# Summing the weighted values of a graph convolution on TensorE instead of halving them on VectorE, with a reordered step and more buffers in the expert FFN

## The chip, the cores and the metric

The kernel runs on one core of one Trainium2 chip. The core has the engines that the profile names PE (TensorE, matrix products), DVE (VectorE), ACT (ScalarE), POOL (GpSimd) and SP (SyncE, which here only issues transfers), and sixteen DMA engines. The metric is the device time of one launch in microseconds; the time given is the median of several runs.

## The reference

The program is a two-layer graph network on 3125 nodes of 256 features and 100,000 edges, all in fp32. Each layer adds a graph convolution and a mixer to the nodes and then a feed-forward part. Layer 0, cut to what matters here:

```python
def transformer_conv(x, edge_index, wq, bq, wk, bk, wv, bv, ws, bs, heads, out_ch):
    ...
    qi, kj, vj = (q[dst], k[src], v[src])
    alpha = jnp.sum(qi * kj, axis=-1) / math.sqrt(out_ch)
    amax = jax.lax.stop_gradient(jax.ops.segment_max(alpha, dst, num_segments=n))
    ex = jnp.exp(alpha - amax[dst])
    denom = jax.ops.segment_sum(ex, dst, num_segments=n)
    alpha = ex / denom[dst]
    out = jax.ops.segment_sum(vj * alpha[..., None], dst, num_segments=n)
    out = out.reshape(n, heads * out_ch)
    return out + x @ ws + bs
...
h = transformer_conv(x, edge_index, w1q, ...)
h = leaky_relu(batch_norm(h, g1, be1))
h = transformer_conv(h, edge_index, w2q, ...)
...
topk_vals, topk_idx = jax.lax.top_k(gate_logits, K)      # 16 experts, K = 2
topk_w = jax.nn.softmax(topk_vals, axis=-1)
h = jax.nn.relu(jnp.einsum('bsh,ehf->bsef', x, w1) + b1)
expert_out = jnp.einsum('bsef,efh->bseh', h, w2) + b2
sel = jnp.take_along_axis(expert_out, topk_idx[:, :, :, None], axis=2)
y = x + jnp.sum(topk_w[..., None] * sel, axis=2)
return (y - mu) / jnp.sqrt(var + EPS) * gamma + beta     # mu, var: of y, per row
```

So for every node, each of its incoming edges fetches the key and the value of its source node; a softmax over the node's edges (4 heads of 64) weighs the values, and the weighted values are summed. This is done twice, with a batch norm between. Independently of it a mixer of four layers (linear attention, then an MLP of 256 to 1024 to 256) runs on the same normalized input. The two results are added to x, and each row goes to its two best experts.

## The kernel before, in words

**The convolution.** Nodes are sorted by their number of edges into 25 blocks of 128 (one node per partition). A block has as many slots as its busiest node has edges: `SLOTS` (L627) lists 64, 43, 41 down to 22, 833 in all. `steps` (L912) cuts a block into sub-blocks of at most `SUB` = 8 slots (L630) and pairs them into steps; over both convolutions there are 126 steps and 230 sub-blocks, 80 of 8 slots, 126 of 7 and 24 of 6. `SlotOrder` (L1063) does the work of a step:

- `gathers` (L1076): one indirect DMA by POOL per slot (issued in `gather`, L635) brings 128 rows of key and value from `kvtab` into `kv`; the pool of `kv` has four buffers, two steps' worth, and gathers run one step ahead.
- `keys`: DVE multiplies keys by the query (L1114) and reduces (L1117); `softmax` and `exp` (L1141, ACT) make the weights.
- `values` (L1147 to L1158): DVE multiplies the values by the weights (L1153) and then adds the second half of the sub-block's slots onto the first (L1158).
- `sums` (L1160): PE adds what is left by matmuls with the identity, which accumulate in the PSUM tile `cps` (L1168) over all sub-blocks of a step:

```python
left = [*range(m // 2), *range(m // 2 * 2, m)]
for j in left:
    self.k.nc.tensor.matmul(
        t["acc"][:, :D], self.k.ident, kv[:, j, D:], start=(b0 + j == 0),
        stop=(b == len(t["subs"]) - 1 and j == left[-1]),
    )
```

  So 8 slots take 4 matmuls, 7 take 4 and 6 take 3.
- `result` copies the sum out (L1175, ACT); `join` and its parts put a block's steps together.

**The order.** PE, DVE and ACT run this stage in an order written out by hand (`PATTERN`, L1060, under `manual_schedule`, L1364): the letters are the parts above, and at each of three `m` per step a `Filling` (L838) puts in pieces of the mixer's work, measured out by their PE time. `l0_gnn_slots` (L1318) runs the two convolutions and tells the filling how many such points there are. While the mixer is in an attention part, few matmuls and much DVE work lie beside the convolution; in an MLP part (L1855, L1873), many matmuls. The same sum in layer 1 (`by_slots`, L942, halves at L1020 and matmuls at L1023) is a function of its own.

**The expert FFN** (`l0_ffn_routed`, L2034). For seven groups of up to four tiles of 125 tokens, the gate's logits, the two best experts and the place of each token in its expert's list are worked out (slot numbers `sloti`, L2132). Then 50 indirect DMAs by POOL scatter the tokens' rows to the experts' lists `xs` in DRAM (L2135); a zero fill of `xs` comes before them. The normed rows `acc` are made with gamma, and beta is added to `xcur` by seven POOL instructions (L2148), which the scheduler put ahead of the scatters. The loop over 16 experts (L2152 on) waits for all scatters (`after`, L291, adds a wait by hand), loads `xe`, transposes it, multiplies by the two weights and writes the rows `ys`. In the combine each token tile gathers its two result rows (`g`, L635, from a pool `f_back` of 8 buffers), DVE adds them with their weights (L2196) and normalizes, and the group is stored (`x`, rows, columns) with the layer-1 keys and values (`st`, L2220, stored to `kvtab` by SP).

Of the kernel before, what the change touches and what calls it, by code (L numbers as in the profile page):

```python
# [14 lines left out]
ALU = mybir.AluOpType  # L15
# [4 lines left out]
P = 125  # L20
D = 256
# [269 lines left out]
def after(k, ins, others):  # L291

    for other in others:
        k.tc.add_manual_dep(
            ins.ins, other.ins.name,
            mybir.DependencyInfo(mybir.DependencyClass.Sync, mybir.DependencyReason.DATA),
            reason="rows of the table",
        )
# [295 lines left out]
def l0_gnn(k, x, conv, y_mix, xcur):  # L594
# [32 lines left out]
SLOTS = [  # L627
    64, 43, 41, 39, 38, 37, 36, 35, 35, 34, 33, 33, 32, 32, 31, 30, 30, 29, 29, 28, 27, 26, 25, 24, 22
]
# [282 lines left out]
def steps(ns):  # L912

    n = -(-ns // SUB)
    subs = [ns // n + (i < ns % n) for i in range(n)]
    return [subs[i : i + 2] for i in range(0, n, 2)]
# [146 lines left out]
class SlotOrder:  # L1063
# [79 lines left out]
    def values(self, n, b):  # L1143

        nc, t, H = self.k.nc, self.steps[n], self.HEADS
        if b == 0:
            nc.vector.tensor_reduce(  # L1147
                self.tile(t["i"])["den"][:, t["c"]], t["w"].rearrange("p s h -> p h s"), axis=AX.X,
                op=ALU.add,
            )  # L1150
        m, kv, b0 = t["subs"][b], t["kv"][b], sum(t["subs"][:b])
        v = self.heads(kv[:, :m, D:])
        nc.vector.tensor_tensor(  # L1153
            v, v, t["w"][:, b0 : b0 + m].unsqueeze(3).to_broadcast([128, m, H, D // H]), op=ALU.mult
        )
        half = m // 2
        v = kv[:, :half, D:]
        nc.vector.tensor_tensor(v, v, kv[:, half : 2 * half, D:], op=ALU.add)  # L1158

    def sums(self, n, b):  # L1160

        t = self.steps[n]
        m, kv, b0 = t["subs"][b], t["kv"][b], sum(t["subs"][:b])
        if b == 0:
            t["acc"] = self.pp.tile([128, 512], F32, name="cps", tag="cps")
        left = [*range(m // 2), *range(m // 2 * 2, m)]
        for j in left:
            self.k.nc.tensor.matmul(  # L1168
                t["acc"][:, :D], self.k.ident, kv[:, j, D:], start=(b0 + j == 0),
                stop=(b == len(t["subs"]) - 1 and j == left[-1]),  # L1170
            )

    def result(self, n):
# [144 lines left out]
def l0_gnn_slots(k, dram, order, a, y, pp, pq, cw, filling, tmp):  # L1318
# [4 lines left out]
    nc, N = k.nc, k.N  # L1323
    NQ = len(SLOTS)
# [7 lines left out]
    with ExitStack() as st:  # L1332
# [11 lines left out]
        for g0, ng in k.groups:  # L1344
            t = wp.tile([P, 4, 2 * D], F32, name="st", tag="st")
# [14 lines left out]
    bmv = cw.tile([128, 2, 2], F32, name="bmv")  # L1360
    sc = cw.tile([128, 2], F32, name="sc")
    sh = cw.tile([128, 2], F32, name="sh")
    mix = filling(2 * 3 * sum(len(steps(n)) for n in SLOTS) + NQ)
    with k.tc.manual_schedule(engines=ORDERED):  # L1364
        mix.ahead(30.0)
        prev = None
        for n in (1, 2):
            if n == 2:
                weights = l0_qs_weights(k, cw, a, 2)
            wq, bq, wsk, bs, gam, bet = weights  # L1370
# [85 lines left out]
            with ExitStack() as st:  # L1456
# [4 lines left out]
                sent, ps = [], None  # L1461
                norm_cols(k, h[:, 0], h[:, 0], sc, sh)
                for i in range(NQ):
# [8 lines left out]
                    if n == 1:  # L1472
                        mix(0.3)
                        t = wp.tile([128, 2 * D], F32, name="kvrow", tag="kvrow")
                        nc.vector.tensor_tensor(t, ps, bkv, op=ALU.add)
                        put_rows(k, kvtab2, order, i, t, sent)
                    else:
                        t = wp.tile([128, D], F32, name="row", tag="row")
# [434 lines left out]
def layer0(k, dram, x, order_of, a, y):  # L1913
# [3 lines left out]
    with ExitStack() as st:  # L1917
        wts, one, mwp, hp, hp2, cw, pp, cp, pq = pools(
            k, st,
            [("m_w", 1), ("m_one", 1), ("m_work", 1), ("m_hid", 1), ("m_hT", 2), ("c_w", 1)],  # L1920
            [("m_ps", 4), ("c_ps", 2), ("c_qa", 2)],
        )
        for g0, ng in k.groups:
            nc.sync.dma_start(y[:, g0 : g0 + ng], tok(x)[:, g0 : g0 + ng])
        tmp = ExitStack()
        order = order_of(pools(k, tmp, [("n_one", 1), ("n_wk", 4)]), cp)
        with ExitStack() as s2:
            (wp,) = pools(k, s2, [("m_ln", 1)])
            mv, rs = ln_stats(k, wp, y)
            for i in range(NT):  # L1930
                ln_tile(k, y[:, i], y[:, i], mv, rs, i)
        pieces = l0_mix_pieces(k, dram, sub("L0_mix_"), y, wts, one, mwp, hp, hp2, pp)
        gout, sent = l0_gnn_slots(
            k, dram, order, sub("L0_gnn_"), y, cp, pq, cw, lambda n: Filling(pieces, n), tmp
        )
        (wp,) = pools(k, st, [("c_add", 2)])
        for g0, ng in k.groups:
            xt = wp.tile([P, 4, D], F32, name="xt", tag="xt")
            part = wp.tile([P, 4, D], F32, name="part", tag="part")
            nc.sync.dma_start(xt[:, :ng], tok(x)[:, g0 : g0 + ng])  # L1940
            after(k, nc.sync.dma_start(part[:, :ng], tok(gout[0:k.N, :])[:, g0 : g0 + ng]), sent)
            nc.gpsimd.tensor_tensor(xt[:, :ng], xt[:, :ng], part[:, :ng], op=ALU.add)
            nc.vector.tensor_tensor(y[:, g0 : g0 + ng], y[:, g0 : g0 + ng], xt[:, :ng], op=ALU.add)
# [90 lines left out]
def l0_ffn_routed(k, dram, xcur, a, over, a1):  # L2034
# [4 lines left out]
    nc, N, NT = k.nc, k.N, k.NT  # L2039
# [9 lines left out]
    with ExitStack() as st:  # L2049
        big, one, wts, wp, gp, bp, hp, pp = pools(  # L2050
            k, st,
            [("f_big", 1), ("f_one", 1), ("f_w", 3), ("f_wk", 3), ("f_g", 2), ("f_back", 8), ("f_hid", 2)],
            [("f_ps", 2)],
        )
        zero = big.tile([128, 4 * D], F32, name="zero")
# [9 lines left out]
        bet = one.tile([P, D], F32, name="bet")  # L2065
# [23 lines left out]
        sent = []  # L2089
        for g0, ng in k.groups:  # L2090
# [7 lines left out]
            for j in range(ng):  # L2098
                at = ps[:P, j * NE : j * NE + NE]
                for c in range(2):  # L2100
                    m = nc.tensor.matmul(
                        at, xT[:, c, j * P : j * P + P], gw[:, c, :], start=(c == 0), stop=False
                    )
# [29 lines left out]
            for i in range(g0, g0 + ng):  # L2133
                for r in range(2):
                    ins = nc.gpsimd.indirect_dma_start(  # L2135
                        out=xs, in_=acc[:, i], in_offset=None,
                        out_offset=bass.IndirectOffsetOnAxis(ap=sloti[:, r, i : i + 1], axis=0),
                    )
# [6 lines left out]
        nc.vector.tensor_reduce(over[:P, 0:1], full, axis=AX.X, op=ALU.max)  # L2145
        for g0, ng in k.groups:
            x = xcur[:, g0 : g0 + ng]
            nc.gpsimd.tensor_tensor(x, x, bet.unsqueeze(1).to_broadcast([P, ng, D]), op=ALU.add)  # L2148

        b1 = one.tile([128, NE, 4], F32, name="b1")  # L2150
        nc.sync.dma_start(b1, a["b1"].rearrange("e (c p) -> p e c", p=128))
# [38 lines left out]
        for gi, (g0, ng) in enumerate(k.groups):  # L2190
# [25 lines left out]
            t = gp.tile([P, 4, 2 * D], F32, name="st", tag="st")  # L2216
# [1051 lines left out]
def fast(k, dram, a, out, over, dump):  # L3268

    sub = lambda pre: {s[len(pre) :]: v for s, v in a.items() if s.startswith(pre)}  # L3270

    def show(name, xcur):
        if dump is not None and name in dump:
            k.nc.sync.dma_start(tok(dump[name]), xcur)

    with ExitStack() as st:
        (keep,) = pools(k, st, [("order", 1)])
        order_of = lambda tmp, pp: node_order(
            k, dram, a["src"], a["dst"], keep, tmp, pp, over[:, 0:2]
        )  # L3280
        with ExitStack() as s2:
            (xpool,) = pools(k, s2, [("xcur", 1)])
            xcur = xpool.tile([P, k.NT, D], F32, name="xcur")
            order = layer0(k, dram, a["x"], order_of, a, xcur)
            show("x1", xcur)
            tabs = l0_ffn_routed(k, dram, xcur, sub("L0_ffn_"), over[:, 2:3], sub("L1_gnn_"))
            show("x2", xcur)
        layer1(k, dram, a, out, tabs, order, show)
# [56 lines left out]
```

## Time and profile before

| what | value |
|---|---|
| median of 9 runs | 6414.68 us (6391.49 to 6472.89) |
| profiled execution | 6413.31 us, span 6411.5 us |
| busy share of the span | PE 74%, DVE 68%, POOL 46%, ACT 25% |
| granted TensorE clock, mean | 0.821 of full speed |
| layer 0, convolutions and mixer | about 285 to 3145 us |
| layer 0, beta and routing, scatters | about 3240 to 3370 us |
| layer 0, experts | 3375 to 3620 us |
| layer 0, combine | 3620 to 3793 us, layer 1 behind it |

A group's line gives the line of code, engine, operation, tile written and read, shapes and count; then busy time and the mean of one in ns; then the engine's idle time just before these instructions and what ended most of it. A timeline line gives the start, the duration, the instruction, and in brackets the idle time before it and its releaser. A matmul of fp32 leaves two records, so counts of matmuls in the profile are twice those of the code, and a run of equal matmuls is shown as one line.

### The profile page before, as it was taken

The numbers are of one execution on the slowest core, as the hardware profiler recorded it, in microseconds if no ns is written. First come the engines' busy times: TensorE is split into PE (matmuls) and PEld (weight loads), VectorE is DVE, ScalarE is ACT, GpSimd is POOL, SyncE is SP. The second block draws the span as 40 slices with busy tenths as digits, with TensorE's granted clock in tenths as the row PEclk, the third lists the DMA queues.
The fourth block names the chain that finished last, engine by engine and source line by source line (L and its number), as shares of the span: only waits on it lengthen the run. The fifth ranks groups of instructions, "written<-read, shape, count | busy, mean of one in ns | idle before, by whom it ended". The sixth has DMA issues, their size and how long they took to land. (4 is left out here: it accounts for less than half of the span.)

```text
span 6411.5 us, 48523 instructions
## 1 busy us (share of the span) xinstructions
PE 4740.5 (74%) x15769; PEld 2716.3 (42%) x15769; DVE 4364.0 (68%) x6216; ACT 1584.7 (25%) x3284; POOL 2936.0 (46%) x2945
## 2 busy tenths in 40 slices
PE   3367887688856787678749747787887877787768
PEld 2144554455434555456436423333333333333335
DVE  5287878888488777988531346567777666777657
ACT  1032333322323223322311102222221222221222
POOL 2465665666366565666450233334334434334321
PEclk8687988789878888789859867788887888788879
DMA  5366665666366565666444353334444434344320
GB/s 139 92 180 180 185 184 154 182 190 179 127 176 186 169 177 166 177 188 182 130 143 144 121 182 108 106 107 127 121 121 131 119 112 116 109 121 132 115 68 22
DMA packets 374280, 908.49 MB, mean 142 GB/s; under 512 B 94268, under 2 KB 170074, under 8 KB 373892
## 3 DMA queue, kind: packets, MB, share of 16 engines
q0 software_dynamic: 232624, 725.48, 39.4%
q1 hardware_dynamic: 137412, 168.23, 8.1%
q10 hardware_dynamic: 3982, 11.59, 0.5%
q8 instruction: 128, 2.10, 0.1%
q14 instruction: 134, 1.10, 0.1%
HBM read 813.62 MB, written 91.30 MB: 141 GB/s over the span
## 5 line engine op out<-in xcount | busy, mean ns | idle before, releaser
L635 POOL DMA_INDIRECT kv<-kvtab,slots x2499 | 2462.2, 985 | 2148.6 <-PE acc L1023 859.0
L2599 DVE TENSOR_TENSOR kv<-kv,e 128x1024 f32<-128x1024 f32 (+1 forms) x448 | 504.8, 1139 | 428.7 <-PE e L2594 191.7
L2594 PE MATMUL e<-weT,eaT 128*128 128x512 f32 (+1 forms) x896 | 558.9, 722 | 184.5 <-ACT eaT L2593 102.6
L1168 PE MATMUL cps<-kv,ident 128*128 128x256 f32 x1792 | 527.5, 445 | 134.9 <-DVE kv L1158 70.1
L1114 DVE TENSOR_TENSOR kv<-kv,qa 128x1792 f32<-128x1792 f32 (+2 forms) x230 | 478.7, 2081 | 95.6 <-DMA kv<-kvtab,slots 66.2
L1168 PEld LDWEIGHTS cps<-kv,ident 128*128 128x128 f32 x1792 | 393.2, 226 | 282.0 <-issue 121.2
L1117 DVE TENSOR_REDUCE al<-kv 128x28 f32<-128x1792 f32 (+2 forms) x230 | 479.5, 2085 | 7.9
L1153 DVE TENSOR_TENSOR kv<-kv,qa 128x1792 f32<-128x1792 f32 (+2 forms) x230 | 477.3, 2075 | 0.0
L1873 PE MATMUL mm<-w,hid 128*125 128x256 f32 x1600 | 414.4, 406 | 69.8 <-ACT hid L1863 39.4
L1855 PE MATMUL mm<-hTm,w 128*128 128x500 f32 (+1 forms) x896 | 394.2, 583 | 75.3 <-issue 38.7
L1873 PEld LDWEIGHTS mm<-w,hid 128*125 128x125 f32 x1600 | 309.9, 200 | 156.2 <-issue 65.2
L2594 PEld LDWEIGHTS e<-weT,eaT 128*128 128x128 f32 (+1 forms) x896 | 164.7, 222 | 426.6 <-issue 233.1
L1023 PE MATMUL acc<-kv,ident 128*128 128x256 f32 x896 | 262.7, 456 | 60.5 <-DVE kv L1020 55.5
L1855 PEld LDWEIGHTS mm<-hTm,w 128*128 128x128 f32 x896 | 169.7, 205 | 242.8 <-issue 189.8
L1023 PEld LDWEIGHTS acc<-kv,ident 128*128 128x128 f32 x896 | 203.4, 232 | 142.7 <-DVE kv L1020 87.1
L1545 PE MATMUL mm<-ident,xh 125*128 125x125 f32 x400 | 109.6, 370 | 201.5 <-ACT xh L1535 111.3
L2593 ACT COPY eaT<-e 128x128 f32<-128x128 f32 (+1 forms) x448 | 109.8, 267 | 557.6 <-PE e L2591 281.3
L1158 DVE TENSOR_TENSOR kv<-kv 128x768 f32<-128x768 f32 (+1 forms) x230 | 242.0, 1052 | 7.9
L985 DVE TENSOR_TENSOR kv<-kv,qa 128x1792 f32<-128x1792 f32 (+2 forms) x115 | 238.9, 2078 | 5.0 <-issue 3.8
L989 DVE TENSOR_REDUCE al<-kv 128x56 f32<-128x1792 f32 (+2 forms) x115 | 238.8, 2077 | 5.1 <-issue 4.2
L1014 DVE TENSOR_TENSOR kv<-kv,al 128x1792 f32<-128x1792 f32 (+2 forms) x115 | 235.1, 2082 | 0.0
L2591 PE MATMUL e<-ident,ea 128*128 128x128 f32 (+1 forms) x448 | 133.3, 329 | 97.0 <-issue 41.9
(414 smaller groups left out, 7952.8 us busy)
## 6 DMA issues: line engine op xcount, KB each, us to landing
kv<-kvtab,slots POOLq DMA_INDIRECT x2499
w<-in_L_ffn_w_dram SPq DMA_DIRECT2D x32, 512.0 KB
qd<-qT SPq DMA_DIRECT2D x24, 500.0 KB
kvtab<-st SPq DMA_DIRECT2D x12, 1000.0 KB
qT<-qd SPq DMA_DIRECT2D x24, 500.0 KB
xTg<-xcols SPq DMA_DIRECT2D x24, 500.0 KB
w<-in_L_mix_W_dram SPq DMA_DIRECT2D x8, 1024.0 KB
xs<-zero SPq DMA_DIRECT2D x16, 512.0 KB
```

Source lines behind the costliest of these rows:

```text
L635: return k.nc.gpsimd.indirect_dma_start(out=out, out_offset=None, in_=table, in_offset=bass.IndirectOffsetOnAxis(ap=index, axis=0),)
L985: nc.vector.tensor_tensor(kv[:, :m, :D], kv[:, :m, :D], q.unsqueeze(1).to_broadcast([128, m, D]), op=ALU.mult,)
L1023: nc.tensor.matmul(acc[:, :D], k.ident, kv[:, j, D:], start=(b0 + j == 0), stop=(kv is bufs[-1][2] and j == left[-1]),)
L1114: nc.vector.tensor_tensor(kv[:, :m, :D], kv[:, :m, :D], q.unsqueeze(1).to_broadcast([128, m, D]), op=ALU.mult)
L1117: nc.vector.tensor_reduce(t["al"][:, b0 : b0 + m], self.heads(kv[:, :m, :D]), axis=AX.X, op=ALU.add)
L1153: nc.vector.tensor_tensor(v, v, t["w"][:, b0 : b0 + m].unsqueeze(3).to_broadcast([128, m, H, D // H]), op=ALU.mult)
L1158: nc.vector.tensor_tensor(v, v, kv[:, half : 2 * half, D:], op=ALU.add)
L1168: self.k.nc.tensor.matmul(t["acc"][:, :D], self.k.ident, kv[:, j, D:], start=(b0 + j == 0), stop=(b == len(t["subs"]) - 1 and j == left[-1]),)
L1855: nc.tensor.matmul(ps[:, :w_], W["w1"][:, c, j * 128 : j * 128 + 128], o["hT"][:, c, :w_], start=(c == 0), stop=(c == 1),)
L1873: nc.tensor.matmul(ps[:P, :D], s["hid"][:, c, j * P : j * P + P], W["w2"][:, c, :], start=(c == 0), stop=False,)
L2594: nc.tensor.matmul(e[:, :n].rearrange("p b d -> p (b d)"), eaT[r], weT[r, :n].rearrange("p b d -> p (b d)"), start=True, stop=True,)
L2599: nc.vector.tensor_tensor(t, t, e[:, :n].unsqueeze(2).to_broadcast([128, n, 2, D]), op=ALU.add)
```

## The change

```diff
@@ values
-        half = m // 2
-        v = kv[:, :half, D:]
-        nc.vector.tensor_tensor(v, v, kv[:, half : 2 * half, D:], op=ALU.add)
@@ sums
-        left = [*range(m // 2), *range(m // 2 * 2, m)]
-        for j in left:
+        for j in range(m):
             self.k.nc.tensor.matmul(
                 t["acc"][:, :D], self.k.ident, kv[:, j, D:], start=(b0 + j == 0),
-                stop=(b == len(t["subs"]) - 1 and j == left[-1]),
+                stop=(b == len(t["subs"]) - 1 and j == m - 1),
             )
@@ l0_gnn_slots
-    mix = filling(2 * 3 * sum(len(steps(n)) for n in SLOTS) + NQ)
+    mix = filling(2 * 3 * sum(len(steps(n)) for n in SLOTS) + 1 * NQ)
@@ l0_ffn_routed
-            [("f_big", 1), ("f_one", 1), ("f_w", 3), ("f_wk", 3), ("f_g", 2), ("f_back", 8), ("f_hid", 2)],
+            [("f_big", 1), ("f_one", 1), ("f_w", 3), ("f_wk", 3), ("f_g", 2), ("f_back", 14), ("f_hid", 2)],
@@ l0_ffn_routed
-            nc.gpsimd.tensor_tensor(x, x, bet.unsqueeze(1).to_broadcast([P, ng, D]), op=ALU.add)
+            ins = nc.gpsimd.tensor_tensor(
+                x, x, bet.unsqueeze(1).to_broadcast([P, ng, D]), op=ALU.add
+            )
+            after(k, ins, sent[-1:])
```

The weighted values of all of a sub-block's slots go to PE, and no halves are added on DVE. Of the number of filling points only the spelling changes. In the FFN the pool of gathered result rows has fourteen buffers, and each beta add waits for the last scatter.

In the compiled program PE, DVE and ACT keep their order of instructions otherwise; DVE has 230 fewer, PE 770 more matmuls (1666 instead of 896). On POOL the seven beta adds stand behind the fifty scatters and behind a partition all-reduce, with the library switch that used to come before an iota of layer 1 now ahead of them. Two POOL gathers of layer 1's edge features (`ea`), issued among the combine's 50 gathers, stand behind 26 and 30 of them instead of 16 and 20, and the first 14 gathers have no wait for a buffer, where 8 had none.

## Prediction

> **What bounds the kernel now.** I read the share of busy time, then the windows by stage, the waits inside layer 0, and single timeline rows. Most of the change lies in layer 0's two convolutions with the mixer beside them (300 to 3140 us). Its windows (columns: us, busy and count of PE, PEld, DVE, ACT, POOL, then PE clock, DMA share, GB/s):
>
> ```profile
> 300.00:600.00 300.00, 193.97 (x672) 129.47 (x672) 245.53 (x335) 89.12 (x199) 184.13 (x184) 0.76 0.61 178
> 600.00:1000.00 400.00, 341.87 (x1296) 233.31 (x1296) 330.38 (x436) 119.70 (x219) 257.59 (x261) 0.91 0.63 182
> 1000.00:1300.00 300.00, 205.70 (x749) 138.86 (x748) 256.90 (x392) 98.86 (x227) 176.37 (x178) 0.78 0.60 174
> 1300.00:1640.00 340.00, 283.80 (x1011) 187.30 (x1009) 273.80 (x357) 90.23 (x159) 221.28 (x223) 0.89 0.62 180
> 1780.00:2100.00 320.00, 210.05 (x752) 139.71 (x753) 272.94 (x378) 103.69 (x235) 194.33 (x193) 0.79 0.61 179
> 2100.00:2470.00 370.00, 302.24 (x1146) 207.53 (x1145) 282.81 (x362) 107.09 (x187) 217.95 (x222) 0.88 0.60 174
> 2470.00:2820.00 350.00, 253.69 (x915) 170.25 (x914) 306.84 (x448) 118.81 (x273) 210.48 (x210) 0.82 0.60 176
> 2820.00:3140.00 320.00, 265.85 (x967) 179.41 (x966) 252.03 (x331) 90.99 (x161) 187.85 (x188) 0.89 0.59 172
> 800.00:900.00 100.00, 89.12 (x337) 60.16 (x335) 85.92 (x111) 29.19 (x49) 66.43 (x68) 0.95 0.64 181
> ```
>
> Two kinds of stretch alternate with the mixer's layers. **A**, beside attention (300, 1000, 1780, 2470; 1270 us): PE 863 busy (68%), DVE 1082 (85%). **B**, beside the mixer's MLP (the other four; 1430 us): PE 1194 (83%), DVE 1139 (80%). The last line is the stage's densest 100 us: PE 89%, clock 0.95. Neither engine is full; they hand sub-blocks to each other:
>
> ```profile
> POOL kv L635 <- PE cps L1168: 323.7, 69, 17.8
> PEld cps L1168 <- DVE kv L1158: 92.6, 37, 12.9
> DVE kv L1114 <- DMA kv<-kvtab,slots: 66.2, 23, 20.0
> ```
>
> (us, times, longest; window 300 to 3140.) Gathers wait for the sums to free a buffer, DVE only 66 us for gathers. The page's chain of waits ends its walk about 5.12 ms, after this stage, so I followed releasers back by the page's rule from the stage's last work. Of 2840 us: PE 943, DVE 902, issue 404, POOL 186, ACT 151. The sums (L1168) have 71 of their 239.9 busy us on it in A (30%) and 157 of 281.8 in B (56%); the halves (L1158) 42 of 106.9 in A and 35 of 132.4 in B.
>
> **The change, part by part.**
>
> ```profile
> L1168 PE MATMUL cps<-kv,ident 128*128 128x256 f32 x1792 | 527.5, 445 | 134.9 <-DVE kv L1158 70.1
> L1158 DVE TENSOR_TENSOR kv<-kv 128x768 f32<-128x768 f32 (+1 forms) x230 | 242.0, 1052 | 7.9
> 837.58 1.89 PE L1168 MATMUL cps<-kv,ident 128*128 128x256 f32 x8
> 839.31 1.84 PE L1855 MATMUL mm<-hTm,w 128*128 128x500 f32 x4
> 1102.96 3.78 PE L1168 MATMUL cps<-kv,ident 128*128 128x256 f32 x8 [1.78 <-DVE kv L1158]
> 1106.53 1.40 PE L1419 MATMUL cps<-ident,res 128*128 128x128 f32 x6
> ```
>
> (1) *Sums.* A matmul leaves two records, so 1792 records are 896 matmuls. The 230 sub-blocks (80 of 8 slots, 126 of 7, 24 of 6) go from 4, 4, 3 matmuls to 8, 7, 6: 320 + 378 + 72 = 770 more. By 384 recorded matmuls in A and 500 in B these split 330, 430 and 10 elsewhere. Price: start to next start of four is 839.31 - 837.58 = 1.73 us, 0.43 each, at full clock, and 1106.53 - 1102.96 = 3.57, 0.89, at half. Group means: 0.625 in A, 0.563 in B. Added PE: 142 (0.43) to 206 (0.625) in A, 185 to 242 in B.
>
> (2) *Halves.* 230 DVE instructions go: 106.9 us in A, 132.4 in B. The instruction order of PE, DVE and ACT is otherwise unchanged.
>
> (3) *On the path.* B, by shares: 56% of 185 to 242 is 104 to 136, less the halves' 35: +69 to +101. B, by room: if PE reaches the densest window's 89%, (1194 + 185) / 0.89 = 1549, +119; with the old busy also shrinking to that window's clock, (1194 x 0.893 / 0.95 + 185) / 0.89 = 1469, +39 (0.893: B's mean clock). I take **+75**, near the shares' lower end, since added matmuls follow one another without a wait. A: 30% of 142 to 206 is 43 to 62, less 42: +1 to +20; DVE loses its part while PE has 407 idle us there, so I take **0**. Bounds for A: -107 (every half on the path, no sum on it) to +62 (the reverse). For B: -35 to +183, (1194 + 242) / 0.89.
>
> The clock's records here stand at 0.5 or 1.0 only, averaging 0.76 to 0.82 in A and 0.88 to 0.91 in B, 0.99 in the experts' stage (PE 98% busy): denser means warmer. [...]
>
> (4) *Beta behind the scatters.*
>
> ```profile
> 3288.63 2.34 POOL L2148 TENSOR_TENSOR xcur<-xcur,bet 125x1024 f32<-125x1024 f32 x1 [7.42 <-DVE acc L103]
> 3291.97 0.73 POOL L2148 TENSOR_TENSOR xcur<-xcur,bet 125x256 f32<-125x256 f32 x1 [1.00 <-DVE acc L103]
> 3293.09 1.22 POOL L2135 DMA_INDIRECT xs<-acc,sloti  x1 [0.39 <-issue]
> ...
> 3366.42 1.19 POOL L2135 DMA_INDIRECT xs<-acc,sloti  x1 [0.30 <-issue]
> ```
>
> Fifty scatters now queue behind the last of seven adds, (3366.42 - 3293.09) / 49 = 1.50 us apart, and the experts' first read follows them. Without the adds they start when rows and slot numbers are ready. Those of the seven groups come at 3274.2, 3286.9, 3300.9, 3311.7, 3321.9, 3328.9 and 3332.3; eight scatters take 12 us, so the ends run 3286.2, 3298.9, 3312.9, 3324.9, 3336.9, 3348.9, 3351.9 instead of 3367.6: **-15** (bounds -21, back to back from the end of the zero fill at 3272.1, and 0). The experts keep PE 239 of 245 us busy, so the gain passes through them whole. The seven adds (some 15 us) and a library switch ahead of them go where POOL idles, until 3620; the first add waits for the last scatter to land, and what is queued behind it (six adds, then a memset of layer 1 that now runs at 3620) is wanted by nobody sooner. If the landing came so late that POOL entered the combine with the adds unfinished, it would cost at most their 15 us.
>
> An add met by DVE work costs DVE: L1971, normally 0.2 us, took 2.33 beside the 2.34 us add. [...]
>
> (5) *Fourteen buffers.* The combine (3620 to 3793) lets more result gathers run ahead.
>
> ```profile
> 3723.05 0.69 DVE L2220 TENSOR_TENSOR st<-mm,bkv 125x512 f32<-125x512 f32 x1 [16.17 <-DMA kvtab<-st]
> ```
>
> Once gathers have led, DVE waits for the stores of its own results; gathers ahead of it don't shorten that: **0**. Bounds: -20, POOL's longest wait for a buffer there (19.14 us, by its waits), and +5, because two loads for layer 1 fall ten gathers (15 us) further back on POOL, where nothing reads them before 3785.
>
> **Sum.** The profiled run took 6413.3 (span 6411.5; the median, 6414.7, is 1.4 above). 6413.3 + 75 + 0 - 15 + 0 = **6473**.
>
> **Rivals.** *R1, faster:* DVE sets A's pace, sums hide in PE's 407 idle us. A -107, B +17 (half of the 104 that the shares give its sums, less the halves' 35), -15: 6308; with half of A's part 6362. For: DVE 85% busy in A. Against: 42 of 107 us on the path. It decides when over half of A's halves come off and under a fifth of its added sums stays on.
>
> *R2, PE becomes the bound in B:* it saturates without warming: +119 to +183, A +20 to +62, -15: 6537 to 6643, likeliest 6545. For: PE leads B already, and later sums free buffers later (the 324 us wait). Against: denser is warmer.
>
> *R3, both hidden:* only (4) shows: 6398. For: 404 us of issue on the path that no engine owns. Against: 157 us of sums on it in B.
>
> That the change doesn't do what it says: the compiled order shows 1666 matmuls for 896 and no halves, so only (5) can be empty.
>
> **How the numbers follow.** Forecast 0.40, R1 0.20, R2 0.22, R3 0.18. The forecast's own range is 6437 (B +39) to 6537 (B +119, A +20). The range 6375 to 6560 takes in R3 and R2's likeliest time, and leaves out most of R1 and R2's tail, 2 in 10. A measurement of this kernel can tell about 0.5% (6381 to 6445) from no change: faster 0.22 (R1, a corner of R3), same 0.21 (rest of R3, the forecast's low end), slower 0.57.
>
> **What would show it.** Right: no L1158 group; L1168 at x3332 and 800 to 960 us; B's windows at 88% PE or more, some 75 us longer in all, A's as long as before; DVE under 80% in A; the first scatter at once after its slot numbers and the experts 15 us earlier after them; the combine still waiting on kvtab<-st. Wrong: A's windows much shorter (R1), B's clock unchanged and 120 us longer (R2), or both as they were (R3).

## The result, and the profile after

The changed kernel takes 6449.95 us (median of 20 runs, 6414.03 to 6468.86) against 6412.42 for the kernel before (62 runs, 6372.18 to 6472.89): ratio 1.0059, 95% interval 1.0045 to 1.0074, some 38 us slower. The forecast was 6473, 60 us slower.

The profiled execution took 6472.5 us (span 6470.7), which is 59 us over that of before. Not all of it belongs to the change, as the lengths of the stages show. I cut both traces at the first product of the convolutions (line L1114), the end of their last values (L1153; before the change the last halves, L1158), the end of the first slot numbers, the experts' first transpose, their last result, and the last key and value rows of the combine:

| stage, us | before | after | difference |
|---|---|---|---|
| convolutions with the mixer | 2829.7 | 2884.4 | +54.7 |
| from there to the first slot numbers | 146.4 | 148.1 | +1.7 |
| first slot numbers to first expert | 99.7 | 82.4 | -17.3 |
| experts | 246.2 | 247.1 | +0.9 |
| combine | 165.1 | 165.5 | +0.4 |
| layer 1 | 2626.3 | 2646.4 | +20.1 |

Up to the end of the combine the change costs 39 us, which is what the medians say. Layer 1, whose code is the same but for the place of two loads, differs by 20 us; over the eleven profiles of this study on chips of the same speed its length lies anywhere from 2626 to 2672, whatever the kernel. It is the runs' spread.

The page's group of the sums now stands at (busy, mean of one, idle before):

```profile
L1164 PE MATMUL cps<-kv,ident 128*128 128x256 f32 x3332 | 844.1, 408 | 65.1 <-issue 45.9
```

The records rise from 1792 to 3332, the busy time by 317 us, 0.41 us for each of 770 matmuls: the price of the full clock (0.43), not that of the group's old mean (0.59). The halves' group is gone. The next two fences are the windows of before and after, cut this time where the mixer turns from attention to MLP and back (the first and last of its MLP activations), so that each line holds about the same work in both (the second MLP part is cut at 1644 and 1667, near the end of the first convolution); the columns are those of the prediction.

```profile
559.00:944.00 385.00, 331.60 (x1244) 225.67 (x1244) 306.49 (x385) 112.09 (x194) 256.67 (x260) 0.90 0.64 182
944.00:1260.00 316.00, 214.74 (x776) 143.00 (x774) 274.77 (x431) 105.87 (x250) 176.29 (x178) 0.78 0.58 172
1260.00:1644.00 384.00, 318.75 (x1154) 212.35 (x1154) 309.96 (x400) 106.81 (x185) 249.52 (x252) 0.89 0.62 179
1766.00:2065.00 299.00, 181.78 (x662) 122.04 (x663) 259.14 (x353) 90.08 (x214) 180.60 (x180) 0.77 0.61 180
2065.00:2456.00 391.00, 323.34 (x1215) 220.33 (x1214) 296.67 (x370) 114.56 (x199) 239.71 (x244) 0.89 0.60 172
2456.00:2772.00 316.00, 221.71 (x796) 148.11 (x795) 276.13 (x423) 107.36 (x255) 182.43 (x183) 0.80 0.60 178
2772.00:3127.00 355.00, 292.06 (x1062) 198.79 (x1061) 288.93 (x370) 102.93 (x182) 218.51 (x219) 0.89 0.60 173
298.00:559.00 261.00, 163.49 (x575) 110.94 (x576) 221.19 (x310) 76.40 (x179) 158.44 (x159) 0.76 0.61 179
```

```profile
553.00:960.00 407.00, 369.58 (x1454) 264.70 (x1453) 272.26 (x351) 112.49 (x194) 247.83 (x261) 0.93 0.61 173
960.00:1280.00 320.00, 244.68 (x968) 171.75 (x968) 251.79 (x409) 106.51 (x251) 170.36 (x178) 0.85 0.57 170
1280.00:1667.00 387.00, 347.90 (x1363) 249.25 (x1362) 272.23 (x363) 106.14 (x184) 239.08 (x251) 0.94 0.61 178
1795.00:2110.00 315.00, 209.96 (x815) 147.93 (x816) 236.59 (x331) 90.02 (x213) 171.28 (x180) 0.80 0.59 171
2110.00:2491.00 381.00, 353.59 (x1435) 255.89 (x1434) 260.54 (x334) 114.59 (x200) 230.48 (x242) 0.97 0.61 176
2491.00:2819.00 328.00, 245.73 (x950) 172.00 (x949) 250.24 (x399) 108.37 (x256) 172.13 (x180) 0.85 0.58 170
2819.00:3181.00 362.00, 323.38 (x1290) 232.26 (x1289) 256.39 (x336) 103.19 (x181) 211.09 (x222) 0.95 0.59 172
297.00:553.00 256.00, 181.98 (x701) 130.19 (x702) 200.12 (x290) 75.93 (x179) 151.52 (x158) 0.82 0.62 181
```

Added up, A (beside attention) goes from 1192 to 1219 us, PE busy from 782 to 882, DVE from 1031 to 939, the clock from 0.78 to 0.83. B (beside the MLP) goes from 1515 to 1537 us, PE from 1266 to 1395 (91%), DVE from 1202 to 1061, the clock from 0.89 to 0.95. One pair of profiles is not enough to say which of the two pays more: cut in the same way, but with the second MLP part taken to the end of the first convolution's values (1656 and 1680 here), the four profiles of this study with the convolutions of before have A between 1191 and 1217 us and B between 1516 and 1527, the three with all slots summed (on chips of the same speed) A between 1210 and 1220 and B between 1549 and 1558. On average A grows by 16 us, B by 36, and the piece between the convolutions by 5. B's growth is clear of that spread; A's alone is not.

What waits for the sums has grown. First the waits of before, then of after (window of the whole stage; us, times, longest):

```profile
POOL kv L635 <- PE cps L1168: 323.7, 69, 17.8
...
ACT res L1175 <- PE cps L1168: 52.8, 21, 6.1
...
DVE xcur L1881 <- PE cps L1168: 6.5, 4, 3.6
```

```profile
POOL kv L635 <- PE cps L1164: 363.0, 83, 20.6
...
ACT res L1171 <- PE cps L1164: 129.8, 45, 7.2
...
DVE xcur L1877 <- PE cps L1164: 38.7, 8, 8.9
```

The copy of a step's result, the mixer's residual add and the next gathers all wait longer for the sums than they did. Of the copies' wait, 16 to 25 us lay in A in the four profiles of before and 42 to 44 in the three of all slots summed; the gathers' longer wait is in B alone. The scatters come next. Before, these were the first slot numbers and the experts' first transpose (the first scatter, at 3293.09, stands in the prediction):

```profile
3274.04 0.15 DVE L2132 CAST sloti<-slot 125x8 int32<-125x8 f32 x1
3373.90 1.33 PE L2166 MATMUL tp<-ident,xe 128*128 128x128 f32 x5 [42.61 <-DMA xe<-xs]
```

After, POOL's scatters, and the experts behind them:

```profile
3330.68 1.21 POOL L2131 DMA_INDIRECT xs<-acc,sloti  x1 [30.29 <-DMA b<-in_L_ffn_b_dram]
...
3404.48 1.18 POOL L2131 DMA_INDIRECT xs<-acc,sloti  x1 [0.30 <-issue]
```

```profile
3411.82 1.97 PE L2165 MATMUL tp<-ident,xe 128*128 128x128 f32 x8 [26.65 <-DMA xe<-xs]
```

The scatters start 1.3 us after the first slot numbers (3329.4), 18.9 us after them in the kernel before, and still run at one per 1.5 us.

### The profile page after: what moved, and what is told of

Same layout as the page of the kernel before. It is cut to its first block, busy times and chain, and to the rows that moved or that the text cites. A ratio compares the mean times of both kernels' runs of the same rounds, so it can differ in the third digit from the quotient of the medians.

```text
span 6470.7 us, 51416 instructions
## 1 busy us (share of the span) xinstructions
PE 4978.9 (77%) x17309; PEld 2963.2 (46%) x17309; DVE 4122.5 (64%) x5986; ACT 1585.8 (25%) x3284; POOL 2863.7 (44%) x2945
## 5 line engine op out<-in xcount | busy, mean ns | idle before, releaser
L635 POOL DMA_INDIRECT kv<-kvtab,slots x2499 | 2394.0, 958 | 2259.5 <-PE acc L1023 867.4
L1164 PE MATMUL cps<-kv,ident 128*128 128x256 f32 x3332 | 844.1, 408 | 65.1 <-issue 45.9
L1164 PEld LDWEIGHTS cps<-kv,ident 128*128 128x128 f32 x3332 | 681.3, 207 | 242.6 <-issue 109.6
L1114 DVE TENSOR_TENSOR kv<-kv,qa 128x1792 f32<-128x1792 f32 (+2 forms) x230 | 478.8, 2082 | 103.8 <-DMA kv<-kvtab,slots 69.1
L1153 DVE TENSOR_TENSOR kv<-kv,qa 128x1792 f32<-128x1792 f32 (+2 forms) x230 | 475.5, 2075 | 0.0
L1869 PE MATMUL mm<-w,hid 128*125 128x256 f32 x1600 | 400.2, 398 | 29.9 <-issue 25.1
L1851 PE MATMUL mm<-hTm,w 128*128 128x500 f32 (+1 forms) x896 | 375.1, 562 | 60.3 <-DVE xcur L1877 25.3
L1859 ACT ACTIVATE hid<-mm,b 128x500 f32<-128x500 f32 (+1 forms) x224 | 133.2, 632 | 267.3 <-PE mm L1851 205.7
```

What stands on the lines that cost most here:

```text
L635: return k.nc.gpsimd.indirect_dma_start(out=out, out_offset=None, in_=table, in_offset=bass.IndirectOffsetOnAxis(ap=index, axis=0),)
L1114: nc.vector.tensor_tensor(kv[:, :m, :D], kv[:, :m, :D], q.unsqueeze(1).to_broadcast([128, m, D]), op=ALU.mult)
L1153: nc.vector.tensor_tensor(v, v, t["w"][:, b0 : b0 + m].unsqueeze(3).to_broadcast([128, m, H, D // H]), op=ALU.mult)
L1164: self.k.nc.tensor.matmul(t["acc"][:, :D], self.k.ident, kv[:, j, D:], start=(b0 + j == 0), stop=(b == len(t["subs"]) - 1 and j == m - 1),)
L1851: nc.tensor.matmul(ps[:, :w_], W["w1"][:, c, j * 128 : j * 128 + 128], o["hT"][:, c, :w_], start=(c == 0), stop=(c == 1),)
L1869: nc.tensor.matmul(ps[:P, :D], s["hid"][:, c, j * P : j * P + P], W["w2"][:, c, :], start=(c == 0), stop=False,)
```

## The experiments

The twelve runs were made on chips of two speeds. The kernel before took 5898 us on the chip of three of them (B alone, and the first runs of the added sums and of no halves), called the faster chip below, and 6435 to 6446 on the slower chips of the other nine; the last section returns to it. Ratios are to the kernel before on the same chip; percentages compare better than microseconds.

**The parts alone.** The sums and halves as changed, the rest as before (the cut shows what differs from the changed kernel):

```diff
-            [("f_big", 1), ("f_one", 1), ("f_w", 3), ("f_wk", 3), ("f_g", 2), ("f_back", 14), ("f_hid", 2)],
+            [("f_big", 1), ("f_one", 1), ("f_w", 3), ("f_wk", 3), ("f_g", 2), ("f_back", 8), ("f_hid", 2)],
...
-            after(k, ins, sent[-1:])
```

> Layer 0's sums and halves as in the changed kernel, beta and buffers as before. Theory (the convolutions pay, the scatters give back): +54 us, the growth of the convolution stage in the changed kernel's profile, so 6467. Rival (part of the changed kernel's loss is in layer 1, by the moved loads and buffers): no more than +37, the whole change's loss.

> The sums part alone once more, on one chip with the next two. Theory: +0.7%, the convolution stage 2% longer, as in its first run. If the price hangs on the chip: another ratio than 1.007 where before's own time differs.

Measured: 1.0071 (1.0047 to 1.0096) and 1.0080 (1.0053 to 1.0107), some 46 to 51 us; the convolution stage took 2890.8 and 2881.0 us. With the changed kernel's own 2884.4 the three average 2885.4, and four profiles of kernels whose convolutions are those of before (2829.7, 2819.3, 2825.4, 2842.5) average 2829.2. The sums part costs 56 us there, more than the whole change, as the theory had it. The ratios alone would not decide that, since their intervals overlap that of the whole change; the stage lengths leave nothing for layer 1 to have added.

Beta behind the scatters, alone (the diff's last part):

> Only the beta adds behind the scatters. Theory: -16 us, all of it between the last slot numbers and the first expert, 6397. Rival (the adds beside the experts block DVE and give the gain back): 0, with the experts' stage some 15 us longer than 245.

> The kernel before with only the beta adds behind the scatters, the one part that the profiles show to gain, as the version that should beat both kernels. Theory: 82.5 us instead of 99.7 from the first slot numbers to the first expert, so -17 us, 0.25 to 0.3% on either kind of chip. Rival: the runs' own spread, mostly layer 1's, hides it, and the ratio's interval holds 1.

Measured: 0.9982 (0.9957 to 1.0007) and 0.9966 (0.9942 to 0.9990). The first interval holds 1, the second does not. The two profiles agree on the place: 82.8 and 82.6 us from the first slot numbers to the first expert, where 99.7 was the rule, so -17. The experts took 245.9 and 247.3 us, 246.2 before: nothing is given back there. From the first of these runs, POOL and then DVE:

```profile
3343.45 0.39 POOL L3305 PARTITION_ALL_REDUCE worst<-over  x1 [5.60 <-issue]
3351.24 14.58 POOL L2148 TENSOR_TENSOR xcur<-xcur,bet 125x1024 f32<-125x1024 f32 x7 [7.40 <-issue]
```

```profile
3355.60 0.42 DVE L2189 TENSOR_TENSOR ye<-o,b 128x256 f32<-128x256 f32 x1 [8.63 <-PE o L2185]
3357.32 0.42 DVE L2189 TENSOR_TENSOR ye<-o,b 128x256 f32<-128x256 f32 x1 [1.30 <-PE o L2185]
3359.05 0.42 DVE L2189 TENSOR_TENSOR ye<-o,b 128x256 f32<-128x256 f32 x1 [1.30 <-PE o L2185]
```

The seven adds run in one piece of 14.6 us beside the experts, and DVE's adds in that time take the 0.42 us that they take without it. In the kernel before, single DVE instructions took some 2 us beside such an add: of the routing L1971 with 2.33 (median 0.22), L1980 with 2.19 (0.16) and L1977 with 2.11 (0.22), of the norm L103 with 2.44 (0.41). Neither routing nor norm lies beside the adds any more:

```profile
3288.72 2.33 DVE L1971 TENSOR_TENSOR oh<-oh,io 125x64 f32<-125x64 f32 x1
```

Why those took longer beside an add and the experts' do not, no run here shows.

The buffers alone:

> Only fourteen buffers for the gathered results. Theory: 0 (within 5), the combine as long as before, 165 us from the first gather to the last kvtab row. Rival (layer 1 pays for the two later loads, the 20 us that its part was longer in the changed kernel's profile): +20.

Measured: 1.0004 (0.9982 to 1.0026); the combine 164.8 us, 165.1 before. The rival's +20 us (1.0031) lies outside that interval. POOL did stop waiting for buffers, and then waited elsewhere. POOL's waits in the combine, before and then with fourteen buffers:

```profile
POOL xg L635 <- DMA kvtab<-st: 47.7, 1, 47.7
POOL g L635 <- DVE ln_mv L2011: 30.3, 6, 19.1
```

```profile
POOL xg L635 <- DMA kvtab<-st: 74.0, 1, 74.0
...
POOL g L635 <- DVE acc L2196: 4.7, 6, 3.2
```

POOL no longer waits for a buffer (30.3 us, now 4.7) and waits as much longer for the stored rows at the combine's end.

**Where the sums cost.** All slots summed, and no halves, in one kind of stretch only (`in_mlp` is the list of steps beside the MLP; the other kernel has `return in_mlp`):

```diff
+        if self.whole(n):
+            return
         half = m // 2
...
+    def whole(self, n):
+        beside = (range(10, 30), range(43, 63)) if self.conv == 0 else (range(12, 32), range(45, 63))
+        in_mlp = n in beside[0] or n in beside[1]
+        return not in_mlp
...
         left = [*range(m // 2), *range(m // 2 * 2, m)]
+        if self.whole(n):
+            left = [*range(m)]
```

> All slots summed on TensorE and no halves only in the steps beside the mixer's attention (92 of 230 sub-blocks, 323 matmuls more), the rest as before. By the changed kernel's stage lengths: A +27, so 6439. By the prediction's step: 0. Rival R1 (DVE sets A's pace): -50 to -107.

> All slots summed on TensorE and no halves only in the steps beside the mixer's MLP (137 of 230 sub-blocks, 444 matmuls more), the rest as before. By the changed kernel's stage lengths: B +22 to +28, so 6438. By the prediction's step: +75, so 6488. Rival R2: +119 or more.

Measured: A alone 1.0036 (1.0011 to 1.0061), 23 us, its convolution stage 2856.2, 27 over the average of before. B alone 1.0038 (1.0025 to 1.0050), 22 us, on the faster chip. (The traces count 91 sub-blocks and 319 added matmuls for the first kernel, 139 and 451 for the second, a little other than expected.) On the slower chips the whole sums part takes 56 us of stage and A alone 27, which leaves 29 for B. So both pay, and neither R1 (A faster) nor R2 (B 119 us or more) is there on the slower chips. Which stretch A's loss falls into stays open: A alone has 1204 us in A, 4 over the average of before, and 1542 in B, 23 over it, though B's own steps are nearly those of before.

**Halves and sums apart.** First sums for all slots with the halves kept, then no halves with the old number of sums (the first counts the second halves twice, the second leaves them out, so that each shows one price alone):

```diff
-        left = [*range(m // 2), *range(m // 2 * 2, m)]
+        left = [*range(m)]
```

```diff
-        half = m // 2
-        v = kv[:, :half, D:]
-        nc.vector.tensor_tensor(v, v, kv[:, half : 2 * half, D:], op=ALU.add)
```

> The price of the sums alone: the halves stay on VectorE and TensorE sums all slots as well (the second halves are then counted twice). Theory (halves have 77 us of the path before, and so hide that much of the sums' price): +54 + 77 = +131, so 6544. Rival (the halves are hidden): +54.

> What the halves cost by themselves: no halves, and TensorE sums only as many slots as before (the second halves' values are left out). Theory, by the halves' share of the path: -77 us, so 6336. Rival R1 (DVE sets the pace): -107 in A alone, up to -239. Rival (hidden): 0.

> No halves and only as many slots summed as before (values left out), beside the sums part alone: the difference of the two is the price of the 770 matmuls once VectorE has been freed. Theory: it is well over the price that they had with the halves in place (1.4%): 1.007 - 0.9725, some 3.4%. Rival (the two parts are independent): 1.4%, so no gain over before of more than 0.7% here.

> Halves kept and all slots summed (second halves counted twice), on one chip with the two before. Theory: +1.4%, as in its first run, so that taking the halves off on top of it is worth 0.7%. Rival (independent parts): 1.007 + 2.75% = +3.4%.

| ratio (interval) | chip at 5898 us | chip at 6437 us |
|---|---|---|
| sums for all slots, halves kept | 1.0138 (1.0119 to 1.0157) | 1.0132 (1.0101 to 1.0164) |
| no halves, sums as before | 0.9725 (0.9702 to 0.9748) | 0.9962 (0.9938 to 0.9986) |
| both (the sums part) | not run there | 1.0080 (1.0053 to 1.0107) |

The first surprise is the price of the halves: 162 us on the one chip, 24 on the other, where their share of the path had given 77. The sums alone cost 81 and 85 us, between the theory (+131) and its rival (+54). My theory that sums and halves hide each other, so that the sums cost 3.4% once the halves are gone, fell with it: on the slower chip they then cost 1.2%, and by the run times the parts are near independent (-0.4% + 1.3% = +0.9%, measured +0.8%), as the rival had it. By the stage lengths they are less so (-50 and +75 us make +25, together they take +56), from one profile each; to some 30 us this stays open.

On the faster chip the two prices sum to -1.4%, and neither the full sums part nor A alone was run there. B alone (451 of the 770 matmuls) cost +0.38%, and that doesn't settle it. The three traces of that chip, cut as above, have these lengths:

| us, faster chip | A | B |
|---|---|---|
| B alone (A as before) | 1164 | 1340 |
| sums for all slots, halves kept | 1186 | 1391 |
| no halves, sums as before | 1079 | 1260 |

In A the sums cost 22 there and the halves were worth 85. In B, taken as 1318 before (1340 less the 22 us that B alone cost), the sums cost 73 and the halves were worth 58, which makes +15 where +22 was measured. If they add in A as they nearly do in B, A would gain some 60 us, and the whole sums part would be some 40 us faster than the kernel before on that chip. That is an estimate from single profiles; it means that R1 is ruled out on the slower chips only.

Whole-stage windows on the slower chips: no halves, then sums added.

```profile
300.00:3080.00 2780.00, 2129.29 (x7800) 1440.73 (x7801) 2047.89 (x2928) 863.36 (x1755) 1632.00 (x1704) 0.85 0.60 178
```

```profile
300.00:3203.00 2903.00, 2386.60 (x9329) 1689.45 (x9330) 2286.19 (x3155) 863.52 (x1755) 1682.13 (x1704) 0.89 0.58 170
```

The same window of before:

```profile
300.00:3127.00 2827.00, 2143.46 (x7796) 1436.78 (x7797) 2282.26 (x3153) 861.53 (x1755) 1695.45 (x1703) 0.84 0.60 175
```

DVE loses 234 us and the stage about 50 of them. PE's nominal 770 x 0.43 = 331 us arrive as 243 (2143 to 2387): the clock goes from 0.84 to 0.89, and the old work shrunk by that ratio plus the added is 2143 x 0.84 / 0.89 + 331 = 2354. The stage takes about 75.

**One step the other way.** Each sub-block folded down to two slots on DVE:

```diff
-        half = m // 2
-        v = kv[:, :half, D:]
-        nc.vector.tensor_tensor(v, v, kv[:, half : 2 * half, D:], op=ALU.add)
+        while m > 2:
+            lo = (m + 1) // 2
+            v = kv[:, : m - lo, D:]
+            nc.vector.tensor_tensor(v, v, kv[:, lo:m, D:], op=ALU.add)
+            m = lo
...
-        left = [*range(m // 2), *range(m // 2 * 2, m)]
+        left = [0, 1]
```

> One step the other way: VectorE folds each sub-block twice, down to 2 slots, and TensorE sums those two: 436 matmuls fewer (80 x 2 + 126 x 2 + 24), some 190 us of TensorE at 0.43, and 230 adds more, some 150 us of VectorE by the halves' 0.96 us at 768 and 1.23 at 1024 elements. If the prices measured away from the kernel before hold this way too (halves taken off alone: 0.67 us per us of VectorE; sums added alone: 0.25 us per us of TensorE): 150 x 0.67 - 190 x 0.25 = +55, the kernel before is near the best split. If TensorE leads, as in the changed kernel (24 for VectorE, -117 for TensorE by 0.16 and 0.62): -93.

Measured: 1.0061 (1.0039 to 1.0084), 39 us slower, nearer to the first theory's +55 than to the other's -93; the convolution stage 2867.5, +38. Its window and its sums:

```profile
300.00:3165.00 2865.00, 2027.32 (x6941) 1322.32 (x6942) 2427.59 (x3384) 860.71 (x1759) 1708.39 (x1703) 0.81 0.59 172
```

```profile
L1170 PE MATMUL cps<-kv,ident 128*128 128x256 f32 x916 | 320.1, 482 | 235.6 <-DVE kv L1159 160.4 <-issue 63.8 <-ACT hid L1865 11.2
```

Of 436 x 0.43 = 188 us taken from PE, 116 come off (2143 to 2027): the clock falls from 0.84 to 0.81, and 2143 x 0.84 / 0.81 - 188 = 2034. A record of the sums that are left takes 0.48 us on average instead of 0.45. The sums now wait 160 us for the folds, 70 before. On the slower chips halving once is the best of the three splits: more work for PE costs, and more for DVE costs. On the faster chip neither other split was run.

The version that beats both kernels is the one before with only the beta part: the two runs above, -0.2% and -0.3%, of which the second alone is clear of no change; the 17 us in both profiles bear it out.

## Why the prediction was right

- *Sign and size.* Forecast +60, measured +38 (ratio 1.0059), inside the forecast's own range. That the total came so near is in part luck: the two steps below were off in opposite directions. Of the signs that were named, the sums' group (844 us), PE at 91% in B, DVE at 77% in A and the scatters came; B some 75 us longer and A as long as before did not.
- *The step on the path, B* was mis-sized: +75 forecast, +22 in the aligned pair and +36 on average. Of its two ways the room with a warmer clock (+39) was near, and the shares (+69 to +101) were not. B's clock rose to 0.95 throughout, not in its densest 100 us alone: the old work shrunk by 0.8925 / 0.947 plus 444 x 0.43 is 1384 us of PE, measured 1395. Going near the shares gave that away.
- *The step on the path, A* failed: "I take 0", measured +23 with the change in A alone (interval 7 to 39). PE had 407 idle us in A and DVE lost 92, but PE keeps its written-out order, and the added sums stand ahead of work that others wait for; the result copies' wait for them in A grew from some 20 to some 43 us. That idle time in total was no room at the place is how I read this, and no run tests it.
- *Shares of the path as prices* were too high both ways on chips like that of the profile: sums 147 to 198 us by the shares, 75 to 85 measured alone; halves 77, measured 24 (runs) to 50 (stage). On the faster chip the halves were worth 162. One reading, not tested, is that what leaves the chain is followed by the next chain, and what joins it finds slack.
- *Scatters*: -15 forecast, -17 measured, by the mechanism as described. *Buffers*: 0; the ratio measured was 1.0004, the combine 0.3 us shorter.
- *The clock*: that denser means warmer held, with B going from 0.89 to 0.95 as PE went from 84% to 91% busy. B was 22 to 36 us longer all the same. On the faster chip B alone brought the clock in B to 0.99 and PE to 98% busy, and still cost 22 us.

## What to carry to other kernels

When work moves from one engine to another and neither is full, measure each half by itself, and don't price it by its busy time or its share of the chain: here 331 nominal us of TensorE cost 75 to 85, and 242 us of VectorE were worth 24 to 162. TensorE's clock buffered both ways here: with the added matmuls it went from 0.84 to 0.89, with the removed ones to 0.81. Compare stages cut at the same work: the two profiles' 59 us fell apart at once into +55, -17 and 20 us of spread in code that had not changed. And take several profiles before you say which stretch pays, and more than one chip before you say that a split of the work is the best.

## What was not expected

Chips differ. The kernel before took 5898 us on one chip and 6412 to 6446 on the others. The experts took 247 us on both kinds; the convolutions (2618 with B's sums, against 2856 with A's) and layer 1 (2333 to 2352, against 2626 to 2672) did not. ACT's waits in the convolution stage, of the kernel before and then of the one with the sums added on the faster chip:

```profile
ACT hid L1863 <- remote: 91.8, 15, 10.7
ACT hid L1863 <- PE mm L1855: 90.6, 33, 7.1
ACT qa L1141 <- issue: 89.6, 11, 24.1
```

```profile
ACT hid L1863 <- PE mm L1855: 159.8, 64, 9.8
ACT o L1433 <- PE cps L1425: 158.2, 21, 13.3
ACT res L1175 <- PE cps L1168: 142.5, 51, 6.6
```

In the first of these profiles ACT stands 573 us (119 times) in waits that end in nothing the trace shows ("issue" and "remote"). On the slower chips it is 426 to 585 us in each of the eleven profiles, and of the some 90 longer than 1 us, 40 to 60 fall on the same instructions in any two profiles of the same convolutions. On the faster chip there is not one in this stage, and ACT's waits are for PE and DVE. PE and DVE have such waits too (262 and 151 us before, 2 and 8 on the faster chip), so it isn't shown that they start at ACT. All this fits the halves' price: where such stops set part of the pace, a quicker VectorE buys 24 us, and where they are absent, 162. That the stops cause the difference is argued and not shown; what they are stays open.
